# Moving one bitwise OR on VectorE within a head: the look at an ffn weight, from behind the reciprocals to in front of the exits of z

## The chip, the cores and the metric

The kernel runs on one core of one Trainium2 chip. The metric is the device time of one execution in microseconds; lower is better.

## The reference

The input x has 4 batches of 512 tokens with 512 features. It is normalized once (LayerNorm), and the result feeds two branches whose product is added to x:

```
xn = layernorm(x)
# attention: 16 heads of 128, causal
q, k, v = xn @ W_Q + b_Q, xn @ W_K + b_K, xn @ W_V + b_V
p = softmax(where(causal, q @ k.T / sqrt(128), -100000))
s = sum over heads of (p @ v) @ W_O + b_O
# ffn: 1408 inner features, weights of -1, 0 and 1 stored as float32
g = silu((silu(xn @ gate_w.T * gate_s) * (xn @ up_w.T * up_s)) @ down_w.T * down_s)
out = x + s * g
```

All is float32. TensorE multiplies in a format with fewer mantissa bits (`F32R`), so the kernel splits each operand into a high part `hi` and a low part `lo` (what rounding left over) and forms three products, hi·hi, lo·hi and hi·lo.

## The kernel before

**Stages.** An attention stage of 64 heads takes some 955 us, then the ffn takes the rest. The attention stage runs over `heads`, a list of (g, b, i): 8 groups g of two heads, in each group 4 batches b, in each batch the two heads i. The index n in that list numbers the passes of the main loop; n even means i = 0, n odd means i = 1. The whole order is written out by hand (`tc.manual_schedule()`): each engine takes its instructions in the order of the source, and semaphores between engines follow from the data.

**One pass of the loop.** For head n the pass works on three heads at once:

1. `softmax` (L325): TensorE forms the scores `sc`; VectorE adds the mask and takes the row maxima (L351); ScalarE takes the exponential and the row sums (L365); VectorE takes four reciprocals (L368); GpSimd multiplies (L371), which gives `p`.
2. The first half of `fill` (L629): for i = 0 two tiles of v for the group (`psv`, L285 and L289, with VectorE's part at L294 and L295); for i = 1 two tiles of the output projection of the batch before (`pso`, L92 to L94, summed on VectorE at L498 and stored).
3. `turn_p` (L374): VectorE turns `p` in blocks of 32 (L385, six instructions into `sq`), SyncE stores it (`turn`, L390) and loads it back in an order that completes the transposition (`ptr`, four loads, L396). It is used one pass later.
4. `split_p` (L407): the turned P of head n-1 is split: ScalarE makes the high half (L418), VectorE and, for n over 8, GpSimd make the low half (L420). The result is `pt`.
5. `project` (L298) twice, for q and k of head n+1 (`psq` and `psk`, twelve matmuls each at L104). ScalarE adds the bias (L308), VectorE makes the low half (L309).
6. Loads for later passes, issued from ScalarE's queue: sums stored before (`a`, L486), weights (L146), and one ffn weight for the look (L523).
7. `attend` (L438) for head n-1: nine z matmuls (L452, L455, L456). In L452 the order is hi·hi, lo·hi, hi·lo, so the low half of `pt` is first read by the third group of three. Then z leaves PSUM ("the exits of z"): ScalarE writes the high half (L464), VectorE the low half (L465), with two small sums (L475, L476) and a second pair of exits for the last 128 queries.
8. The second half of `fill`.

**The look.** The ffn has two versions. Where all ffn weights are exact in the short format, it can leave the low half of the weights out. The kernel finds this out itself: it loads each of the 33 weight tiles of 128x512 once (11 each of gate, up and down; `load_look`, L516, one per pass from n = 8 on, into a pool of four buffers) and, one pass later, VectorE ORs its bits into a tile `bits` (`look`, L526). After the last, low bits of `bits` decide on the branch. Looks run in passes 9 to 41. In `look`:

```
raw = looking.pop(0)
nc.vector.tensor_tensor(bits, bits, raw.bitcast(I32), ALU.bitwise_or)   # L529
```

**Around the change.** In a pass, VectorE's order is: the maxima (L351), the reciprocals (L368), the look (L529), the first half of `fill`, six turns (L385), the low half of P (L420), the low halves of q and k (L309), the exits of z (L465, L475, L476, L465), the second half of `fill`.

Of the kernel before, what the change touches and what calls it, by code (L numbers as in the profile page):

```python
# [43 lines left out]
def kernel(  # L44
# [67 lines left out]
    with ExitStack() as at:  # L112
# [40 lines left out]
        def flat(s):  # L153
            return Split(s.hi.rearrange("p c e -> p (c e)"), s.lo.rearrange("p c e -> p (c e)"))

        def weight(pool, shape, name, tag):
            return Split(
                pool.tile(shape, F32R, name=name + "h", tag=tag + "h"),
                pool.tile(shape, F32R, name=name + "l", tag=tag + "l"),
            )  # L160
# [15 lines left out]
        def prepare(due, dst, src, name):  # L176

            pending.append((due, dst, stage(src, name)))

        def prepare_qk(h, due, due_k=None):  # L180
            for d, src, n, when in ((wq, w_q, "wq", due), (wk, w_k, "wk", due_k or due)):
                d[h] = weight(wqkp, [P, ND, E], f"{n}{h}", n)
                prepare(when, flat(d[h]), src[h].rearrange("p c e -> p (c e)"), f"{n}r{h}")

        def prepare_v(g, due):
            both = wvop.tile([P, 2, ND, HG * E], F32R, name=f"wv{g}", tag="wv")
            wv[g] = Split(both[:, 0], both[:, 1])
            wv[g].both = both
            half = ND // 2
            for i in range(2):  # L190
                c = slice(i * half, (i + 1) * half)
                src = w_v[g][:, c, :].rearrange("p c e -> p (c e)")
                prepare(due, flat(wv[g][:, c, :]), src, f"wvr{g}_{i}")
# [213 lines left out]
        def split_p(raw, shared):  # L407
            pt = p_split()
            half = NQ // 2
            for k in range(0, NQ, half):  # L410
                src = raw[:, k : k + half].rearrange("p b (s i) -> p b s i", i=Q)

                def dst(part):
                    return part[:, :, k * Q : (k + half) * Q].rearrange(
                        "p s (b i) -> p b s i", i=Q
                    )

                nc.scalar.copy(dst(pt.hi), src)  # L418
                on = nc.gpsimd if shared and k == 0 else nc.vector
                on.tensor_tensor(dst(pt.lo), src, dst(pt.hi32), ALU.subtract)  # L420
            return pt
# [94 lines left out]
        def load_look():  # L516
            if looks:
                k = looks.pop(0)
                src = (gate_w, up_w, down_w)[k % 3][k // 3]
                if k % 3 < 2:  # L520
                    src = src.rearrange("p c i -> p (c i)")
                raw = lnp.tile([P, D], F32, name=f"look{k}", tag="xt")
                nc.scalar.dma_start(out=raw, in_=src)  # L523
                looking.append(raw)

        def look():  # L526
            if looking:
                raw = looking.pop(0)
                nc.vector.tensor_tensor(bits, bits, raw.bitcast(I32), ALU.bitwise_or)  # L529
# [16 lines left out]
        with tc.manual_schedule():  # L546
# [69 lines left out]
            for n, (g, b, i) in enumerate(heads):  # L616
# [23 lines left out]
                of = softmax(qT, kT, norms if n > 0 else [])  # L640
                if n > 0 and early:
                    pt = split_p(raw, B * HG < n < len(heads) - 2)
                look()
                half = NT // 2 if nxt is not None else NT - 1
                fill(range(0, half))
                if n > 0:
# [40 lines left out]
                if g + 1 < NG:  # L687

                    if (b, i) == (1, HG - 1):
                        prepare_qk((g + 1) * HG, (g + 1) * per_g - 2)  # L690
                    if (b, i) == (2, HG - 1):
                        prepare_v(g + 1, (g + 1) * per_g - 1)
                    if (b, i) == (B - 1, 0):
                        prepare_qk((g + 1) * HG + 1, (g + 1) * per_g - 1)
                if g > 0:
                    load_look()
                if before is not None:
# [209 lines left out]
```

## Time and profile before

| | us |
|---|---|
| median of 3 runs | 1212.07 |
| lowest and highest of them | 1211.49, 1213.0 |
| the profiled execution | 1211.04 |
| its span, from first to last instruction | 1209.3 |
| TensorE busy in the span | 1195.7 |
| VectorE busy in the span | 843.6 |
| ScalarE busy in the span | 550.4 |
| GpSimd busy in the span | 377.7 |

The granted TensorE clock was 0.998 of full speed. Lines such as L529 are lines of the kernel before. In a row of the profile the engine (PE is TensorE, DVE VectorE, ACT ScalarE, POOL GpSimd, SP SyncE; a "q" behind the name is its queue of issues) is followed by the operation, by what it writes and reads by the program's names, the shapes, and a count; a row of the timeline begins with start and duration in us, and ends in brackets with the idle time of the engine before it and what ended it.

### The profile page before, as it was taken

What the parts mean: (1) busy time and instruction counts of PE and PEld (TensorE: products, weight loads), DVE (VectorE), ACT (ScalarE), POOL (GpSimd) and SP (SyncE); (2) the same over time, 40 slices, a digit from 0 to 9 for tenths busy, and PEclk for the clock granted to TensorE, in tenths of its full rate; (3) what the DMA queues carried; (4) which work ended last, traced back from release to release, by engine and by line L of the source; (5) the groups of instructions that cost most, each with busy time, mean ns of one, the idle gap of its engine ahead of it and who ended that gap; (6) DMA issues with size and microseconds to landing.
All of it is one profiled execution on the core that took longest, in us unless ns stands there. A gap on an engine that the chain in (4) does not pass through costs nothing.

```text
span 1209.3 us, 18485 instructions
## 1 busy us (share of the span) xinstructions
PE 1195.7 (99%) x6018; PEld 1022.5 (85%) x6018; DVE 843.6 (70%) x2261; ACT 550.4 (46%) x1272; POOL 377.7 (31%) x484
## 2 busy tenths in 40 slices
PE   9999999999999999999999999999999999999997
PEld 8888888888888888888888888888888888888886
DVE  7987777787778877877777777777777543434433
ACT  6654444454445444554544454555444332313231
POOL 3312332343234423432433252325231351202010
PEclk9999999999999999999999999999999999999999
DMA  4465456656675667666766665655555993737241
GB/s 169 141 188 152 137 170 195 208 177 192 192 209 174 199 202 208 186 198 199 204 198 183 184 198 165 189 180 175 175 158 157 287 314 86 215 82 217 79 148 38
DMA packets 117912, 215.52 MB, mean 178 GB/s; under 512 B 13232, under 2 KB 45744, under 8 KB 117808
## 3 DMA queue, kind: packets, MB, share of 16 engines
q1 hardware_dynamic: 73872, 134.38, 36.1%
q10 hardware_dynamic: 29520, 53.40, 14.9%
q0 software_dynamic: 14416, 26.48, 8.0%
q8 instruction: 50, 0.82, 0.3%
q14 instruction: 54, 0.44, 0.1%
HBM read 135.17 MB, written 79.04 MB: 177 GB/s over the span
## 4 chain that ended last, share of the span: by engine, by line
PE 89%; DVE 5%; DMA 4%; ACT 1%; issue 1%; ACTq 0%; SPq 0%; DVEq 0%
PE psq L104 13%; PE psk L104 13%; PE psv L285 8%; PE z L452 8%; PE sc L104 7%; PE pd L770 7%; PE pg L770 7%; PE pu L770 7%; PE pso L92 5%; PE pso L94 4%; PE pso L93 4%; PE psv L289 4%; DMA look<-in_gate_w 1%; DVE sq L385 1%; PE psv L104 1%; DVE pt L420 1%
## 5 line engine op out<-in xcount | busy, mean ns | idle before, releaser
L371 POOL TENSOR_SCALAR p<-p,rtot 128x512 f32<-128x512 f32 (+3 forms) x256 | 148.6, 599 | 595.9 <-DVE rtot L368 572.1
L365 ACT ACTIVATE p<-p,nmax 128x512 f32<-128x512 f32 (+3 forms) x256 | 140.8, 552 | 136.7 <-DVE nmax L351 136.7
L285 PE MATMUL psv<-wv,xh 128*128 128x512 f32 x448 | 124.6, 400 | 0.0
L104 PE MATMUL sc<-k,q 128*128 128x512 f32 (+2 forms) x576 | 112.4, 338 | 1.9 <-DVE xl L261 1.7
L385 DVE STREAM_TRANSPOSE sq<-p 128x256 f32<-128x256 f32 x378 | 113.3, 362 | 0.0
L104 PEld LDWEIGHTS sc<-k,q 128*128 128x128 f32 x576 | 99.0, 188 | 13.5 <-ACT xh L260 1.4
L351 DVE CUSTOM_DVE_ANT_0 p<-sc,mask 128x512 f32<-128x512 f32 (+2 forms) x192 | 96.3, 551 | 0.0
L418 ACT CAST pt<-ptr 128x640 fp32r<-128x640 f32 x126 | 85.1, 724 | 17.7 <-DMA ptr<-turn 11.4
L308 ACT ACTIVATE k<-psk,consts 128x512 fp32r<-128x512 f32 (+1 forms) x65 | 44.3, 682 | 101.7 <-PE psk L104 101.7
L420 POOL TENSOR_TENSOR pt<-ptr,pt 128x640 fp32r<-128x640 f32 x53 | 83.6, 1577 | 13.2 <-ACT pt L418 11.6
L285 PEld LDWEIGHTS psv<-wv,xh 128*128 128x128 f32 x448 | 76.0, 188 | 10.0
L309 DVE SCALAR_TENSOR_TENSOR k<-psk,consts,k 128x512 fp32r<-128x512 f32 (+1 forms) x65 | 48.0, 738 | 45.7 <-ACT k L308 45.4
L796 DVE SCALAR_TENSOR_TENSOR hd<-pu,consts,sg 128x512 f32<-128x512 f32 x44 | 33.0, 751 | 66.3 <-PE pu L770 61.7
L289 PEld LDWEIGHTS psv<-wv,xl 128*128 128x128 f32 x448 | 68.4, 188 | 9.5
L420 DVE TENSOR_TENSOR pt<-ptr,pt 128x640 fp32r<-128x640 f32 x73 | 72.3, 1001 | 2.2 <-ACT pt L418 2.2
L498 DVE TENSOR_TENSOR a<-pso,a 128x512 f32<-128x512 f32 x108 | 69.5, 681 | 2.4 <-DMA a<-acc 1.2
L289 PE MATMUL psv<-wv,xl 128*128 128x256 f32 x448 | 71.0, 280 | 0.0
L368 DVE RECIPROCAL rtot<-tot 128x1 f32<-128x1 f32 x256 | 41.4, 162 | 41.0 <-ACT p L365 34.7
L308 ACT ACTIVATE q<-psq,consts 128x512 fp32r<-128x512 f32 (+1 forms) x65 | 44.2, 680 | 42.3 <-PE psq L104 41.7
L452 PE MATMUL z<-pt,v_0h 128*128 128x512 f32 x128 | 51.1, 399 | 2.8 <-DVE pt L420 2.6
L309 DVE SCALAR_TENSOR_TENSOR q<-psq,consts,q 128x512 fp32r<-128x512 f32 (+1 forms) x65 | 47.6, 732 | 1.2 <-ACT q L308 1.2
L365 ACT ACTIVATION_READ_ACCUMULATOR p<-p,nmax 128x1 f32 x256 | 47.7, 186 | 0.0
(717 smaller groups left out, 3037.2 us busy)
## 6 DMA issues: line engine op xcount, KB each, us to landing
turn<-sq SPq DMA_DIRECT2D x63, 640.0 KB, 2.9
ptr<-turn SPq DMA_DIRECT2D x252, 160.0 KB, 5.0
acc<-a SPq DMA_DIRECT2D x124, 256.0 KB, 2.5
a<-acc ACTq DMA_DIRECT2D x108, 256.0 KB, 3.3
xt<-in_x SPq DMA_DIRECT2D x16, 256.0 KB, 4.1
wor<-in_w_o ACTq DMA_DIRECT2D x16, 256.0 KB, 6.1
fa<-acc SPq DMA_DIRECT2D x16, 256.0 KB, 6.6
fx<-in_x SPq DMA_DIRECT2D x16, 256.0 KB, 6.9
```

Source lines behind the costliest of these rows:

```text
L104: nc.tensor.matmul(ps, l, r, start=n == 0, stop=n == len(todo) - 1)
L285: nc.tensor.matmul(ps, x_[c].hi, wv[g].both[:, :, c, :], start=c == 0, stop=False)
L289: nc.tensor.matmul(ps[:, 1], x_[c].lo, wv[g].hi[:, c, :], start=False, stop=c == ND - 1)
L308: nc.scalar.activation(q.hi[:, at_], ps, AF.Identity, bias=bias[:, h : h + 1])
L309: nc.vector.scalar_tensor_tensor(q.lo[:, at_], ps, bias[:, h : h + 1], q.hi32[:, at_], ALU.add, ALU.subtract)
L351: nc.vector.tensor_tensor_reduce(out=of[t], in0=where[t], in1=add, scale=-SCALE, scalar=BIG, op0=ALU.add, op1=ALU.min, accum_out=nmax[t],)
L365: nc.scalar.activation(of[t], of[t], AF.Exp, bias=nmax[t], scale=-1.0, accum_out=tot)
L371: nc.gpsimd.tensor_scalar(of[t], of[t], rtot, 1.0, ALU.mult, ALU.mult)
L385: nc.vector.transpose(dst.rearrange("p a s i -> p s a i"), src.rearrange("p (s a i) -> p s a i", s=n, i=Q),)
L420: on.tensor_tensor(dst(pt.lo), src, dst(pt.hi32), ALU.subtract)
L452: nc.tensor.matmul(o, v, p_, start=k == 0, stop=k == len(todo) - 1)
L770: nc.tensor.matmul(ps, l, r, start=first and k == 0, stop=last and k == len(pairs) - 1)
```

## The change

The call of `look()` moves from behind `softmax` (and, in early passes, `split_p`) to the place behind the projections of q and k and the loads, in front of `load_look()` and `attend_last()`, which calls `attend`. The load of the next weight tile stays where it was.

```diff
@@ -640,7 +640,6 @@
                 of = softmax(qT, kT, norms if n > 0 else [])
                 if n > 0 and early:
                     pt = split_p(raw, B * HG < n < len(heads) - 2)
-                look()
                 half = NT // 2 if nxt is not None else NT - 1
                 fill(range(0, half))
                 if n > 0:
@@ -692,6 +691,7 @@
                         prepare_v(g + 1, (g + 1) * per_g - 1)
                     if (b, i) == (B - 1, 0):
                         prepare_qk((g + 1) * HG + 1, (g + 1) * per_g - 1)
+                look()
                 if g > 0:
                     load_look()
                 if before is not None:
```

Line numbers between the two places are one lower after the change.

## The prediction

> **What bounds the kernel now.** I read the totals first, then where TensorE stands still, then what VectorE does around that.
>
> ```profile
> span 1209.3 us, 18485 instructions
> PE 1195.7 (99%) x6018; PEld 1022.5 (85%) x6018; DVE 843.6 (70%) x2261; ACT 550.4 (46%) x1272; POOL 377.7 (31%) x484
> ```
>
> TensorE is busy 99% of the span, so only what makes it stand still can be won. A table of two stretches (the answer for stages) shows where that is: while looks run (160 to 626 us) it is busy 463.26 of 466.00 us; when no look is left (670 to 903 us), 233.00 of 233.00.
>
> For a finer count I took from the timeline the start of the first psq matmul of every head n. From 655 us to 918 us those starts lie 14.64 us (to an odd n) and 14.58 us (to an even n) apart, within 0.02 and without exception: a head in which TensorE never waits. Between n = 10 and n = 42 the same steps exceed this by 1.60 (in head 18), 0.78 (22), 0.17 (26), 0.18 (28), 0.88 (31), 0.14 (34), 0.02 (38) and 0.34 us (39). The sum is **4.11 us**, and no other head of that stretch loses anything. These 4.11 us are the whole prize of any change to the looks. The largest case, from the VectorE and TensorE timelines (start, duration, instruction, and in brackets the idle time and its releaser):
>
> ```profile
> 287.32 0.16 DVE L368 RECIPROCAL rtot<-tot 128x1 f32<-128x1 f32 x1 [0.22 <-ACT p L365]
> 287.73 0.95 DVE L529 TENSOR_TENSOR bits<-bits,look 128x512 int32<-128x512 int32 x1 [0.24 <-DMA look<-in_gate_w]
> 288.61 0.41 DVE L294 TENSOR_TENSOR v_rest<-psv,v_0h 128x256 f32<-128x256 f32 x1
> ...
> 290.18 1.80 DVE L385 STREAM_TRANSPOSE sq<-p 128x256 f32<-128x256 f32 x6
> 291.90 1.82 DVE L420 TENSOR_TENSOR pt<-ptr,pt 128x640 fp32r<-128x640 f32 x1
> ...
> 293.87 0.47 PE L452 MATMUL z<-pt,v_0h 128*128 128x512 f32 x1 [1.36 <-DVE pt L420]
> ```
>
> The reader is to see a chain: reciprocals, look, v, transposes, low half of P (pt, L420), and behind it the third group of z matmuls, which needs that low half. VectorE runs it without a gap from the look on, so whatever the look takes is added to the arrival of pt. In a head without a stall (n = 26) pt ends at 411.54 and TensorE goes on at 411.66, with 0.16 us of idle in front of the weight load: the chain has no slack left there.
>
> Then where the look is to go: between the low half of k (L309) and the first exit of z (L465). The same two rows in a head without a look:
>
> ```profile
> 676.19 0.75 DVE L309 SCALAR_TENSOR_TENSOR k<-psk,consts,k 128x512 fp32r<-128x512 f32 x1 [1.61 <-ACT k L308]
> 677.83 0.62 DVE L465 SCALAR_TENSOR_TENSOR z11l<-z,consts,z11h 128x384 fp32r<-128x384 f32 x1 [0.89 <-ACT z11h L464]
> ```
>
> VectorE sits idle 0.89 us there, waiting for ScalarE. And the look itself:
>
> ```profile
> L529 DVE TENSOR_TENSOR bits<-bits,look x33: 692/827/957, 154.3 to 626.0; 128x512 int32<-128x512 int32 x33
>   DMA look<-in_up_w: 1.7, 2
>   DMA look<-in_down_w: 0.9, 2
>   DMA look<-in_gate_w: 0.5, 2
> DMA to landing us min/median/max: 2.9/6.5/8.6
> ```
>
> 33 looks of 0.69 to 0.96 us; six of them also waited for their load, 3.1 us in all.
>
> [...]L420 on VectorE takes 0.77 us at the least and 1.92 at the most, the long ones beside GpSimd's own L420 or L151. [...]
>
> **The change, part by part.**
>
> *What moves.* Only the 33 L529 instructions, n = 9 to 41; in the built program all 33 stand behind L309 of k, and every other engine keeps its order. No DMA is added or moved past another. The loads (L523, on ScalarE's queue) are issued in the same place, one head earlier. Some waits of DMA issues name another earlier transfer, because completion is now seen at another point; those named are the preceding transfers of one head back, so I cost them at nothing (bounds: 0 to 0.3 us either way in all, the size of one 0.34 us issue).
>
> *Removed from the old place.* Each head's chain to pt shortens by what the look held: 0.7 to 0.9 us, plus its wait. Against the eight stalls:
> - Head 18: wait 0.24, and 0.88 from the look's start to the next (288.61 - 287.73), 1.12 together, against a stall of 1.60. 0.48 stays: VectorE is late there for another reason, its z exit of the head before (idle 2.70 us for ScalarE, whose queue issued five loads between 276.90 and 280.42).
> - Head 22: wait 0.64 and 0.83, together 1.47. The high half of pt (L418 on ScalarE, held by the transfer of P) ends at 349.99, so L420 can move from 351.22 to 349.99 only: 1.23, still more than 0.78.
> - Heads 26, 28, 34, 38, 39: at least 0.69 each against 0.34 at most: gone.
> - Head 31: 0.88 from 480.01 to 480.89, against 0.88: gone to within 0.1. The look of head 30 also waited 0.29 us, and behind it the chain of waits runs through the store and reload of P into head 31; that store comes some 1.1 us earlier too.
>
> Sum: 4.11 - 0.48 = **3.63 us won**, with bounds 2.9 (head 18 keeps 1.0 and head 31 keeps 0.3, should L420 be stretched by GpSimd more than now) and 4.11.
>
> *Added at the new place.* Cover: the wait for ScalarE between L309 and L465. Over the heads after the looks this gap is 0.63 to 1.66 us, mostly 0.72 to 0.98; in heads with looks it is now 0.24 to 2.71, the short ones (0.24 in heads 18, 28, 31, 39) in heads that run late because of the look, where k's low half then starts right behind its high half and the gap grows to 0.6 and more. A look of 0.69 to 0.83 us (GpSimd mostly idle here) overhangs by 0.2 us at the most. Behind it wait the exits of z, then v or the sums, then the next head's maxima, so an overhang d makes the next pt later by d; those heads have then 0.7 us and more to give. Cost 0; if the cover is gone (0.83 in full), old and new place cancel, which is the first rival.
>
> *The load's wait.* In head 26 the load was issued at 412.04 and the new place comes at 427.02, 15.0 us later, against a longest landing of 8.6. All 3.1 us of waits go.
>
> **Time.** The profiled execution took 1211.04 us, 1.74 around its span; it would take 1207.4. The median shown, 1212.07, stands 1.03 above it. Taking 3.63 off the median gives 1208.4 us. Two versions of this kernel within 0.2% (2.4 us) can't be told apart.
>
> **Rivals.**
> - *The look stays on the chain* (0.12): it delays the exits of z by its full length, the next maxima by as much, and pt arrives as late as before; only the waits for loads are won. Heads 18, 22 and 38 then gain 0.24, 0.64 and 0.02, head 34 its 0.14: 1.04, giving **1211.0 us**, no change. For it: VectorE is busy 364.62 of 466 us and the gap was 0.24 in four heads. Against: the gap of 0.7 us and more in every head once the look is out of the way, one excepted.
> - *The load holds the exits of z* (0.04, slower): in an even n the low half of z is read by the first sum of the next head; in head 26 it ended at 415.64 and the matmul that reads it starts at 418.29, a margin of 2.65. It decides when a load takes over 15.0 + 2.65 = 17.6 us. A landing of 18 us in all 16 even heads would cost 16 x 0.4 = 6.4 us, **1218.5 us**. Against: no landing over 8.6 us.
> - *The look isn't moved*: excluded by the built order.
>
> **Chances.** The forecast has 0.84, of which 0.04 ends with a gain under 2.4 us. So faster 0.80, same 0.12 + 0.04 = 0.16, slower 0.04. The range goes from 1206.7 (all 4.11 and most of the 1.03 between median and profiled run, should that be load waits) to 1211.0, the first rival's value.
>
> **What would show it.** In the profile after: psq steps of 14.64 and 14.58 us from n = 10 to 42 but for some 0.5 us in head 18; no idle time in front of L529; the gap in front of L465 down to about 0.1 us in most heads; TensorE's waits for pt at L452 (2.6 us) mostly gone. Wrong if L465 starts 0.3 us or more later against psq than now and the eight stalls are still there, or if TensorE waits at L94 for z's low half.

## Result and profile after

The kernel after took 1207.51 us (median of 6 runs, 1206.92 to 1208.75) against 1211.94 us (6 runs, 1211.49 to 1214.62): a ratio of 0.9961, 95% interval 0.9948 to 0.9974. In a later series, beside the last experiments, it took 1207.76 us against 1210.84, ratio 0.9972 (0.9961 to 0.9984). The kernel is faster by 4.4 us in the first series and by 3.1 in the second; the two intervals together run from 1.9 to 6.3 us. 1208.4 was forecast.

The totals of the page of the kernel after:

```profile
span 1207.0 us, 18482 instructions
PE 1194.2 (99%) x6018; PEld 1021.9 (85%) x6018; DVE 841.8 (70%) x2261; ACT 549.8 (46%) x1272; POOL 366.9 (30%) x484
```

While looks run (160 to 626 us) TensorE now never stands still. The table of that stretch, in the kernel before and in the kernel after (us, then for each engine its busy time; clock, DMA share and GB/s at the end):

```profile
160.00:626.00 466.00, 463.26 (x2345) 397.27 (x2344) 364.62 (x1042) 229.95 (x572) 172.05 (x189) 1.00 0.66 196
160.00:626.00 466.00, 466.00 (x2363) 400.83 (x2362) 365.30 (x1049) 230.53 (x573) 164.48 (x192) 1.00 0.66 197
```

The longest of TensorE's waits in the kernel before (who waits for whom, us in total, times, longest) is gone from the list of the kernel after:

```profile
PE z L452 <- DVE pt L420: 2.6, 3, 1.4
```

The idle time (2.74 us) is smaller than what the steps lose, because a short wait does not show as idle: the records of two matmuls that follow each other overlap, by 0.16 us in head 18 of the kernel after, and head 26 lost 0.17 us without an idle row. The span fell by 2.3 us only. What the look touches gained more. From the first psq matmul of head 10 to that of head 42 the kernel before took 471.63 us and the kernel after 467.54, which is 4.09 less. The excess of the steps over 14.64 and 14.58 us, the prediction's measure, is 0.02 us where it was 4.11. The rest lies outside: head 10 starts at 170.37 instead of 168.96 (1.41 later), and from head 42 to the end it takes 569.09 instead of 568.71 (0.38 longer); 4.09 - 1.41 - 0.38 = 2.30. The start of head 10 moves from profile to profile whatever the look does: with the same two kernels it came at 169.36 and 169.13 in later profiles. So the prize is read from the steps, not from one span.

Head 18 again, in the timeline of the kernel after (start, duration, instruction, idle time and its releaser):

```profile
288.03 0.16 DVE L368 RECIPROCAL rtot<-tot 128x1 f32<-128x1 f32 x1 [0.22 <-ACT p L365]
288.29 0.42 DVE L294 TENSOR_TENSOR v_rest<-psv,v_0h 128x256 f32<-128x256 f32 x1
...
289.88 1.80 DVE L385 STREAM_TRANSPOSE sq<-p 128x256 f32<-128x256 f32 x6
291.60 1.20 DVE L420 TENSOR_TENSOR pt<-ptr,pt 128x640 fp32r<-128x640 f32 x1
...
293.76 0.40 PE L452 MATMUL z<-pt,v_0h 128*128 128x512 f32 x1
```

The v part follows the reciprocals at once, pt ends at 292.80, and TensorE reaches the third group of z matmuls 0.96 us later without having waited. In the kernel before, pt ended at 293.72, TensorE stood idle for it for 1.36 us, and the head lost 1.60.

The new place, between k's low half and the exits of z, one head earlier:

```profile
279.03 0.75 DVE L309 SCALAR_TENSOR_TENSOR k<-psk,consts,k 128x512 fp32r<-128x512 f32 x1 [1.59 <-ACT k L308]
279.69 0.68 DVE L529 TENSOR_TENSOR bits<-bits,look 128x512 int32<-128x512 int32 x1
281.79 0.62 DVE L465 SCALAR_TENSOR_TENSOR z4l<-z,consts,z4h 128x384 fp32r<-128x384 f32 x1 [1.41 <-ACT z4h L464]
```

Even with the look in it the gap has 1.41 us of idle time left here. And the look as a tile, with no line of idle time in front of it any more:

```profile
L529 DVE TENSOR_TENSOR bits<-bits,look x33: 681/682/1701, 162.8 to 630.4; 128x512 int32<-128x512 int32 x33
DMA to landing us min/median/max: 2.9/6.5/8.8
```

The loads land as late as before (6.5 us median, 8.8 the longest), but nobody stands waiting for them.

### The profile page after: what moved, and what is told of

Same layout as the page of the kernel before. It is cut to its first block, busy times and chain, and to the rows that moved or that the text cites. A ratio compares the mean times of both kernels' runs of the same rounds, so it can differ in the third digit from the quotient of the medians.

```text
span 1207.0 us, 18482 instructions
## 1 busy us (share of the span) xinstructions
PE 1194.2 (99%) x6018; PEld 1021.9 (85%) x6018; DVE 841.8 (70%) x2261; ACT 549.8 (46%) x1272; POOL 366.9 (30%) x484
## 4 chain that ended last, share of the span: by engine, by line
PE 94%; DVE 3%; DMA 1%; ACT 1%; issue 0%; SPq 0%; ACTq 0%; DVEq 0%
PE psq L104 14%; PE psk L104 14%; PE psv L285 9%; PE z L452 8%; PE sc L104 8%; PE pd L770 7%; PE pg L770 7%; PE pu L770 7%; PE pso L92 5%; PE pso L93 5%; PE pso L94 5%; PE psv L289 4%; PE psv L104 1%; PE sc L342 1%; DVE sq L385 1%; DVE st L213 1%
## 5 line engine op out<-in xcount | busy, mean ns | idle before, releaser
L371 POOL TENSOR_SCALAR p<-p,rtot 128x512 f32<-128x512 f32 (+3 forms) x256 | 135.3, 547 | 603.0 <-DVE rtot L368 578.6
L385 DVE STREAM_TRANSPOSE sq<-p 128x256 f32<-128x256 f32 x378 | 113.4, 365 | 0.0
L418 ACT CAST pt<-ptr 128x640 fp32r<-128x640 f32 x126 | 85.1, 724 | 13.2 <-DMA ptr<-turn 8.5
L309 DVE SCALAR_TENSOR_TENSOR k<-psk,consts,k 128x512 fp32r<-128x512 f32 (+1 forms) x65 | 48.1, 740 | 61.2 <-ACT k L308 60.8
L420 POOL TENSOR_TENSOR pt<-ptr,pt 128x640 fp32r<-128x640 f32 x53 | 83.7, 1579 | 13.3 <-ACT pt L418 10.3
L420 DVE TENSOR_TENSOR pt<-ptr,pt 128x640 fp32r<-128x640 f32 x73 | 69.9, 968 | 3.0 <-ACT pt L418 3.0
L309 DVE SCALAR_TENSOR_TENSOR q<-psq,consts,q 128x512 fp32r<-128x512 f32 (+1 forms) x65 | 47.8, 735 | 3.9 <-ACT q L308 3.9
```

What stands on the lines that cost most here:

```text
L309: nc.vector.scalar_tensor_tensor(q.lo[:, at_], ps, bias[:, h : h + 1], q.hi32[:, at_], ALU.add, ALU.subtract)
L371: nc.gpsimd.tensor_scalar(of[t], of[t], rtot, 1.0, ALU.mult, ALU.mult)
L385: nc.vector.transpose(dst.rearrange("p a s i -> p s a i"), src.rearrange("p (s a i) -> p s a i", s=n, i=Q),)
```

## The experiments

The **theory**: a look's whole time, its duration and its wait, lies on VectorE's chain from the reciprocals to pt, and TensorE waits for pt. The rivals: **only the waits** for loads cost anything; or the look hurts **through GpSimd**, whose multiplication of p runs beside it and is slowed. "Excess" is the sum over n = 10 to 42 of what the steps between heads have over 14.64 and 14.58 us, in the one profile of each version. It is finer than the times, but not free of scatter: two profiles of the kernel before differ by 1.4 us, two of the kernel after by nothing that shows.

| version | excess, us | median, us | ratio to before (95%) |
|---|---|---|---|
| before | 4.11; again 2.73 | 1211.94 | 1 |
| after | 0.02; again 0.02 | 1207.51 | 0.9961 (0.9948 to 0.9974) |
| e1, no look | 0.22 | 1207.50 | 0.9976 (0.9969 to 0.9983) |
| e2, load issued early, old place | 2.46 | 1209.63 | 0.9992 (0.9983 to 1.0001) |
| e3, look in front of pt | 7.77 | 1213.92 | 1.0031 (1.0019 to 1.0042) |
| e4, look behind pt | 0.70 | 1207.92 | 0.9980 (0.9973 to 0.9986) |
| e5, two looks, new place | 1.00 | 1208.72 | 0.9985 (0.9978 to 0.9992) |
| e6, two looks, old place | 13.98 | 1222.32 | 1.0108 (1.0086 to 1.0129) |
| e7, load just ahead of the look | 98.07 | 1303.0 | 1.0765 (1.0731 to 1.0798) |
| e8, VectorE held 0.25 us, old place | 0.29 | 1207.58 | 0.9970 (0.9960 to 0.9980) |
| e9, VectorE held 0.8 us, old place | 2.48 | 1210.44 | 0.9990 (0.9981 to 0.9998) |

Beside the experiments the kernel before took 1210.3 to 1211.2 us. That is why versions without an excess show ratios of 0.997 to 0.998 there.

**One mark for all heads.** The traces show more than the sums. Take the time from a head's first psq matmul to the end of its pt (L420 on VectorE). A head loses what this time has over 6.30 us, and nothing below it. (6.30 is the value that fits. A head without a stall begins its third group of z matmuls 6.52 us behind the first psq, 293.76 - 287.24 in head 18 of the kernel after.)

| version, head | pt ends behind the first psq, us | over 6.30 | lost, us |
|---|---|---|---|
| before, 18 | 7.89 | 1.59 | 1.60 |
| before, 22 | 7.09 | 0.79 | 0.78 |
| before, 26 | 6.45 | 0.15 | 0.17 |
| before, 23 | 6.29 | - | 0 |
| after, 18 | 5.56 | - | 0 |
| e3, 14 | 7.81 | 1.51 | 1.49 |
| e6, 18 | 8.22 | 1.92 | 1.93 |
| e9, 18 | 7.24 | 0.94 | 0.96 |

In the twelve profiles other than e7's this holds within 0.04 us for 382 of the 384 heads from n = 10 to 41; the two others are heads 23 and 39 of e4, which lost 0.2 us more. So what these heads lose is the lateness of pt, whatever made it late.

**The kernel before and after once more.** No edit.

> The kernel before once more, for the spread of its stalls: the steps between heads should again exceed 14.64 and 14.58 us in heads 18 to 39, by 2.5 to 4.5 us in all, with the parts that hang on a load's landing (heads 18, 22, 31) moving most.

> The kernel after once more, on the chip of these runs: excess over the steps under 0.3 us in all; time 2.4 to 4 us under that of before, ratio 0.997 to 0.998, since in the runs beside the experiments before took 1210.3 us and the versions without a stall 1207.5.

Before had an excess of 2.73 us, after 0.02 again. The stalls moved: head 18 lost 0.19 instead of 1.60, head 22 0.04, head 26 0.70, head 31 0.89, head 38 0.59. The size of the prize changes from run to run, its place (VectorE's chain to pt) doesn't. I had expected heads 18, 22 and 31 to move most; head 31 did not move (0.88 and 0.89).

**e1: no look at all.**

```diff
--- after
+++ e1
-                nc.vector.tensor_tensor(bits, bits, raw.bitcast(I32), ALU.bitwise_or)
```

> The kernel after with the 33 looks left out (their loads stay; the bits are never looked at). It says what a look costs at its new place. If the gap in front of the exits of z covers it, nothing: the steps between the first psq matmuls of the heads sum to an excess of 0.0 to 0.1 us over 14.64 and 14.58 us for n = 10 to 42, as in the kernel after (0.04), and the time is 1207.5 us within 0.8. If the look still costs something that the steps do not show, the time falls below 1206.5.

Excess 0.22 us, nearly all of it in head 15 (0.20), and a time equal to that of after. A look at the new place costs nothing that can be measured; there is nothing left to win from the looks.

**e2: the load one head earlier, look at the old place.**

```diff
--- before
+++ e2
-                look()
+                if n > B * HG:
+                    look()
...
-                if g > 0:
+                if n >= B * HG - 1:
                     load_look()
```

> The kernel before with each look's load issued one head earlier (from head 7 on), so that no look waits for its load; the look stays behind the reciprocals. Theory (the look's whole time lies on the chain to pt): only the waits go, 0.24 in head 18, 0.64 in head 22, 0.14 in head 34; an excess of 2.5 to 3.1 us stays of 4.11, time 1210.3 to 1211. First rival (only the waits for loads cost anything): excess under 0.3, time 1207.5 to 1208. Second rival (the look hurts by slowing GpSimd's multiplication beside it): as the theory, 2.5 to 3.1.

Excess 2.46 us. The tile's answer shows that no look waited, and that each lasts as long as before:

```profile
L529 DVE TENSOR_TENSOR bits<-bits,look x33: 818/826/966, 155.0 to 625.2; 128x512 int32<-128x512 int32 x33
```

The waits are therefore 0.3 to 1.6 us of the prize (2.73 or 4.11 less 2.46), and some 2.5 us come with the look's own 0.82 us. With one profile of e2 and 1.4 us between two profiles of before, this split is rough. The times say the same: e2 takes 2.1 us more than e1 beside it and 0.7 less than before. If only waits cost anything, e2 would have e1's time; the first rival has fallen.

**e3 and e4: in front of pt, behind pt.** In both, `look()` leaves its old place.

```diff
--- before
+++ e3
-                look()
...
+                look()
                 if not early:
                     pt = split_p(raw, B * HG < n < len(heads) - 2)
```

```diff
--- before
+++ e4
-                look()
...
                 if not early:
                     pt = split_p(raw, B * HG < n < len(heads) - 2)
+                look()
```

> The look between the turns (L385) and the low half of P (L420): some 4 us later than before, so with hardly a wait for its load, no longer beside GpSimd's multiplication of p, and behind the turns, but still in front of pt. Theory (chain to pt): excess 1.5 to 3 us, time 1209.5 to 1211. Rival of the waits and rival of GpSimd's multiplication: excess under 0.5, time about 1208.

> The look directly behind the low half of P (L420), in front of q's and k's low halves: off the chain to pt, but not in the gap in front of the exits of z. Theory (chain to pt): excess under 0.3, time as after, 1207.5 within 0.8; k's low half starts up to 0.8 us later in heads where q's high half is done, without a stall. If the gap in front of the exits is what matters, an excess of 1 us or more, in heads where k's low half comes late.

One instruction lies between the two places, and 7.77 us of excess against 0.70. In front of pt the look costs more than at the old place, and more than I had expected (1.5 to 3). The timelines of VectorE and GpSimd in head 14 of e3 show why (this head's pt ended 7.81 us behind the first psq):

```profile
232.68 1.87 DVE L529 TENSOR_TENSOR bits<-bits,look 128x512 int32<-128x512 int32 x1
234.47 1.90 DVE L420 TENSOR_TENSOR pt<-ptr,pt 128x640 fp32r<-128x640 f32 x1
232.42 1.58 POOL L420 TENSOR_TENSOR pt<-ptr,pt 128x640 fp32r<-128x640 f32 x1 [2.14 <-ACT pt L418]
233.95 1.73 POOL L151 TENSOR_TENSOR wq4l<-wqr,wq4h 128x512 fp32r<-128x512 f32 x1
```

The look takes 1.87 us instead of 0.68: GpSimd's L420 was running when it began, and it ended 0.55 us behind that one (234.55 and 234.00). L420 on VectorE then takes 1.90 (1.60 in the same head of the kernel before, 0.77 at its shortest there), in the same way behind GpSimd's L151. Head 14 lost 1.49 us. In e4 the looks are stretched too (1.08 us mean), but behind pt this costs little: in heads 23 and 39 a look of 1.77 us delays the low half of q (L309) and TensorE loses 0.2 us behind it.

**e5, e6: two looks.** The same OR again, at the new and at the old place.

```diff
                 nc.vector.tensor_tensor(bits, bits, raw.bitcast(I32), ALU.bitwise_or)
+                nc.vector.tensor_tensor(bits, bits, raw.bitcast(I32), ALU.bitwise_or)
```

> The kernel after with every look done twice at the new place (the same OR again, which changes no bit): 1.36 us against a gap of 0.7 to 2.5. Theory: the overhang of up to 0.65 us delays the exits of z and so the next pt, which has some 1 us to spare in most heads: excess 0 to 1 us, most of it in heads with weights to split (n = 18, 22, 31, 39), time 1207.5 to 1208.5. If the cover is just as long as one look and nothing is to spare behind it, 33 x 0.4 = 13 us.

> The kernel before with every look done twice at the old place. Theory (chain to pt): pt comes 0.8 us later in every head; in the 16 even heads (n = 10 to 40), which had 0.1 to 0.2 us to spare, 0.6 to 0.8 us each, and more in the late odd heads: the excess rises from 4.1 to 13 to 20 us, time 1221 to 1228. Rival (only waits for loads cost): excess stays at 4 to 5.

The same added instruction costs 9.9 us at the old place (13.98 against 4.11, or 11.3 against the second profile's 2.73) and 1.0 us at the new one. At the old place it is nearly always the even heads that pay, which had been expected for want of slack: heads 14, 18, 22, 26, 28, 30, 36 and 38 lost 1.2 to 1.9 us each. At the new place it is heads 24 and 40 (0.60 and 0.33), not 18, 22, 31 and 39, as I had expected: they come one head behind those in which GpSimd splits the weights of v. In those, heads 23 and 39, the second look took 1.66 us (L530 is that second OR; the rows are of head 23):

```profile
367.29 0.71 DVE L529 TENSOR_TENSOR bits<-bits,look 128x512 int32<-128x512 int32 x1
368.04 1.66 DVE L530 TENSOR_TENSOR bits<-bits,look 128x512 int32<-128x512 int32 x1
369.62 0.60 DVE L465 SCALAR_TENSOR_TENSOR z4l<-z,consts,z4h 128x384 fp32r<-128x384 f32 x1
```

L465 shows no idle time in front of it here: the cover is used up, and the next head's chain starts late. Head 24's pt ended 6.88 us behind its first psq.

**e7: the load issued just ahead of its look.** The load now holds the exits of z, as in the prediction's slower rival, but in every head.

```diff
--- after
+++ e7
-                look()
                 if g > 0:
                     load_look()
+                look()
```

> The kernel after with load_look in front of look in the same pass, so that the load is issued just ahead of its look and VectorE waits out its landing, 4 to 7 us, in front of the exits of z. It prices the slower rival of the prediction. Theory: the exits start some 4 us late, over the margin of 2.65 us, and the next pt, which has about 1 us to spare, comes late too: 2 to 4 us for each of the 33 heads, 65 to 130 us, time 1270 to 1340. If the exits of z are not on the path, below 1215.

1303.0 us, 92.6 more than before beside it. This profile's mean granted clock was 0.977, against 0.998 or 0.999 in the others, so a part of the loss may not be the wait's own. From its waits (who waits for whom, us in total, times, longest):

```profile
DVE bits L529 <- DMA look<-in_down_w: 50.3, 11, 9.2
DVE bits L529 <- DMA look<-in_gate_w: 41.9, 8, 7.9
DVE bits L529 <- DMA look<-in_up_w: 41.6, 8, 9.0
PE z L452 <- DVE pt L420: 31.5, 21, 2.3
PE psq L104 <- DVE rest L476: 15.4, 8, 3.4
```

VectorE waited 133.8 us for loads, and TensorE stood still for the next pt, and in front of psq for L476, the sum that reads z from PSUM. The wait that the prediction's rival names, L94 for the low half of z, is there too, but it is small: 5.4 us in 6 times. So the new place is on the path too as soon as something there lasts beyond its cover; a load issued one head earlier keeps it clear of that.

**e8, e9: VectorE held at the old place, with GpSimd not slowed.** The look's OR is left out; reciprocals of one column (128x1) stand in its place.

```diff
--- before
+++ e9 (e8 with range(4))
-                nc.vector.tensor_tensor(bits, bits, raw.bitcast(I32), ALU.bitwise_or)
+                for c in range(13):
+                    nc.vector.reciprocal(held[:, c : c + 1], ones)
```

> The kernel before with each look replaced, at the old place, by four reciprocals of a column of 128x1 (0.16 us each, some 0.85 us from first to next): the look's work on the weights is left out, its loads stay. VectorE is held as long as by a look, but waits for no load[...], so GpSimd's multiplication beside it should not be slowed (L371 135 us in all as in the kernel after, not 148). Theory (time on the chain to pt): an excess of 2 to 3 us, as with the load issued early (2.46). Rival (the look hurts through GpSimd's multiplication): excess under 0.5 us, time as after.

> As the version with four reciprocals in place of each look at the old place, but with thirteen: the four followed each other so closely that they held VectorE for 0.25 us in all (404.06 to 404.31), a third of a look; thirteen should hold it for 0.8 us. The look's work is left out, its loads stay. Theory (time on the chain to pt): an excess of 2 to 3 us, as with the load issued early (2.46), although GpSimd's multiplication is not slowed (L371 at 135 us). Rival (the look hurts through GpSimd's multiplication): excess under 0.5 us.

They separate the theory from the rival through GpSimd, since the look does slow GpSimd: L371, GpSimd's multiplication, was busy 148.6 us in the kernel before, and this is its row in the kernel after and in e9 (busy, mean ns | idle before, releaser):

```profile
L371 POOL TENSOR_SCALAR p<-p,rtot 128x512 f32<-128x512 f32 (+3 forms) x256 | 135.3, 547 | 603.0 <-DVE rtot L368 578.6 <-DVE rstd L239 24.5
```

```profile
L371 POOL TENSOR_SCALAR p<-p,rtot 128x512 f32<-128x512 f32 (+3 forms) x256 | 135.7, 551 | 605.0 <-DVE rtot L368 580.7 <-DVE rstd L239 24.2
```

e8 came out at 0.29 us, which looked like a win for the rival, but it was too small a dose: its four reciprocals overlap and hold VectorE for 0.25 us only, not for the estimated 0.85. e9 has the right one:

```profile
406.25 0.87 DVE L531 RECIPROCAL held<-ones 128x1 f32<-128x1 f32 x13
407.04 0.40 DVE L294 TENSOR_TENSOR v_rest<-psv,v_0h 128x256 f32<-128x256 f32 x1
```

VectorE is held for 0.79 us, GpSimd is not slowed, no load is waited for, and the excess is 2.48 us, about what e2 has with real looks (2.46; so close a match is chance, given 1.4 us between two profiles of one kernel). So the time on the chain is enough to make the stalls. GpSimd's slower multiplication is real, 13.3 us of its busy time (148.6 - 135.3), but none of the turns (L385), which read what it writes, stood waiting in the kernel before while looks ran. The doses also show why the cost is not in proportion: 0.25 us per head costs 0.29 us in all, 0.8 us costs 2.5, 1.6 us (e6) costs 14, because only what passes the mark of 6.30 us counts.

## Why the prediction was right

- *The mechanism* (the look's time lies on VectorE's chain to pt, and TensorE waits for pt) held: e3, e4 and e9, and the mark of 6.30 us, head by head.
- *The prize* (at most 4.11 us, the excess of the steps) held, and e1 shows nothing more to be had. But it was read from one profile; the second one of the kernel before has 2.73.
- *Slack in front of pt.* Head 26, called a head without a stall, is one of the eight (0.17 us). The chain had "no slack left" there, but in the 24 heads without a stall pt had 0.01 to 1.85 us to spare. In seven of the eight that stall, L420 itself was long, 0.94 to 1.89 us, because GpSimd's L151 was running when it began; long ones remain in the kernel after (nine over 1.1 us), where the chain has room for them.
- *Removed from the old place*: forecast 3.63 us won, measured 4.09 in the steps, and 2.71 (2.73 - 0.02) in the second pair of profiles. So the hundredths of the forecast had no meaning, and that the total came so near is in part luck. The term that differs in the first pair is head 18, of which 0.48 us was to stay and nothing stayed. I had taken two things of that head as fixed. The late exit of z of the head before: the two issues of weights in front of it took 2.16 us before and 1.49 after, and the last reciprocal came 0.79 us behind the first psq (288.03 - 287.24) instead of 1.48 (287.32 - 285.84). And L420, 1.82 us before and 1.20 after: it began when GpSimd's L151 had 1.14 us left to run, and in the kernel after 0.53. Neither was fixed, and in the second profile of before the same head lost 0.19.
- *Heads 22, 26, 28, 31, 34, 38, 39*: all gone, as worked out. That the high half of pt (L418) might limit head 22 played no part.
- *Added at the new place*: cost 0, right, by e1 and the kernel after. My overhang of 0.2 us at the most was not: two of the 33 looks took 1.65 and 1.70 us beside GpSimd's splitting of weights, where I had expected GpSimd to be idle. The spare time in front of pt took this up.
- *The gap in front of L465* was to fall to about 0.1 us in most heads. It was 0.2 us or less in 9 of 33 and 0.37 to 1.84 in the others. I had read the gap from heads behind the looks, mostly 0.72 to 0.98; in e1, where nothing fills it, it is 0.53 to 2.58 in the heads of the looks. The cover was larger than forecast.
- *The load's wait*: all gone. The first rival's working gave the waits 1.04 us of the 3.63 and so the duration 2.59; e2 and e9 put the duration at 2.46 and 2.48, one profile each.
- *The rivals.* That the look stays on the chain was wrong by e1. The slower one is real as a mechanism (e7), though its wait at L94 was a small part there, and was rightly kept at 0.04, with no landing over 8.8 us against the 15 us that the load has.
- *The median against the profiled run*: right as a caution. Of the 4.09 us, 1.79 were hidden in the profiled span by the start and the end of the kernel. That two versions within 0.2% can't be told apart was an estimate, and too cautious: with 20 runs, e5's 0.15% is clear of zero.

## What to carry to other kernels

Where one engine is busy 99% of the time, measure the step of its loop where nothing disturbs it and subtract: the excess is the whole prize, and the wait that ends last in the disturbed steps names the chain. Then measure, head by head, when the awaited result arrives: if each loss is the lateness behind one fixed mark, that wait is the cause. Work that nobody waits for belongs where its engine idles for another one's answer, or at the least behind the chain (e4 lost 0.7 us, e3 7.8), not in front of a chain without slack, however idle that engine is on average. And an experiment that puts a delay in must show in its profile that the delay had the intended length before its verdict counts.

## What the runs showed of the hardware that was not expected

- A VectorE OR of two 128x512 SBUF tiles took 0.65 to 0.70 us with GpSimd idle (0.68 in 29 of the 33 looks of the kernel after). Where a GpSimd instruction was running at its start and had over 0.2 us left, the OR ended 0.53 to 0.56 us behind the end of that instruction: in all 191 cases of these profiles, 152 beside a tensor_scalar (31 of them in the kernel before, where the OR took 0.78 to 0.96 us) and 39 beside a tensor_tensor (1.65 and 1.70 us in the kernel after, 1.87 in head 14 of e3). L420 on VectorE, 0.78 us alone, ended 0.68 to 0.69 us behind GpSimd's tensor_tensor in 273 such cases; where the GpSimd instruction had started 0.02 us ahead of it or less (once in the kernel before, twice in the kernel after), L420 took 0.78 to 0.79 us. So the records look as if the VectorE instruction waited for the end of the GpSimd one, and its length says how much of that one was left.
- GpSimd loses in its turn. In the kernel before, the 27 L371 of 128x256 that began during a look took 0.90 to 0.92 us and the others, one excepted, 0.47 to 0.49. In e2 one head's four L371 took 2.48 us, and in e9 2.06. In head 18 of the kernel after, an L151 that began while VectorE's L420 was under way took 1.89 us, and the one before it 1.30.
- Four VectorE reciprocals of 128x1, independent of each other, took 0.33 us from the first start to the last end (e8), and thirteen 0.87 (e9), with 0.14 us shown for each: one every 0.06 us.
